# Two alternating scratch tiles, halved transfers, and layer 1's bias moved from a PSUM seed on ScalarE to an addition on VectorE, in a four-layer graph network

## The chip, the cores and the metric

The kernel runs on one core of a Trainium2 chip. The metric is the device time of one execution in microseconds. Besides it there is one profiled execution, in which every instruction of every engine has a start and an end.

## The reference

Thirty-two graphs go through four layers. A graph has 512 tokens `x` of width 256 and an adjacency `adj` of 512 x 512, everything in fp32. Each layer ends in `x = layernorm(x + layer(x, adj))`. The change touches layer 1 most:

```
layer 0:  relu(((1 + eps) x + adj x) W1 + b1) W2 + b2            (hidden width 512)
layer 1:  h = adj (x W^T + b);   h if h > 0 else alpha h
layer 2:  h = layernorm(x);      relu((adj h) W_rel + b_rel + h W_root), added to x
layer 3:  agg = eps x + adj x;   silu(rmsnorm(agg W1 + b1)) W2 + b2   (hidden width 1024)
```

In layer 1 the sum over the neighbours can be taken first: `adj (x W^T + b) = (adj x) W^T + rowsum(adj) b`. The kernel does it so, and `rowsum(adj) b`, the outer product of row sums and bias, is the term whose place the change moves.

## The kernel before

**Tiling.** A graph's tokens lie in one SBUF tile of 128 partitions x 4 chunks x 256 (a "room", 4 KB a partition; there are 37 of them, line 679). Matmuls are fp32 with 128 x 128 weights and a moving side of 256 or 128 columns. Most products of 2 x 2 blocks are done with seven block products instead of eight (`seven`, line 846), whose operand sums are VectorE's `room<-room` additions, and whose results are added up out of PSUM by VectorE (or copied by ScalarE where it is a first one).

**Transposes.** Layers 0 and 3 end in `dense_turned` (line 1092): the product comes out feature by token, VectorE transposes 32 x 32 squares, and `spread_squares` (line 1272) sends the squares through a scratch buffer in DRAM (`corner`): four transfers of 128 KB into it, one of 512 KB back (line 1282). `add_turned` (line 1131) then adds the result to `x` in two halves, each of which reads from the whole returned tile. Layer 2 needs its input turned and goes the like way with `gather_squares` (line 1285): four transfers out, four of 128 KB back. All these transfers are issued by SyncE, in order.

**Norms.** `Norm.half` (line 1177) lets ScalarE take sums and sums of squares of two chunks of 256: the activation's own output is not wanted and goes to one tile, `scrap` (line 836, written by `total`, line 735), only its accumulator counts. GpSimd takes the power -0.5 (`inv_sqrt`), and `Norm.put` (line 1210) scales each chunk on VectorE or on ScalarE, whichever the planner picks.

**Layer 1** (line 1398). With `SEED = 1` ScalarE first writes `b_1` times the row sum of each token into the PSUM bank (line 1421), two instructions for each half, and the matmuls of `dense_tok` (line 997) accumulate on top. Then ScalarE takes `relu(-ps)`, and VectorE makes the leaky activation and the residual with two scalar_tensor_tensor instructions (lines 1431 and 1432).

**The order of the work** is not left to a scheduler of the language. Every operation is recorded (`Plan.do`, `Plan.move`) with its operands and a cost from small formulas (lines 33 to 95): busy time and latency for the engines, wire time and lateness for the transfers. `Plan.order` (line 479) then plays the kernel through with these costs: always the operation that can start first, among those by rank, the rank being graph number times `period` plus due time (`RULES`, `SHIFT`); a tile or bank is taken when the plan holds it free. Up to five graphs are in flight (`FLIGHT`). It fixes, for all 32 graphs, the order of instructions on each engine, the tile each uses, and, where an operation has two ways, the engine (`YIELD` is a surcharge on VectorE there). `SPARE` is added to the landing of each transfer, `AHEAD` limits how far a later graph may run ahead. The instructions are issued in this order (line 1567); so every constant among these moves instructions of the whole kernel. Nearly all instructions are issued at line 366, all transfers at line 413.

Of the kernel before, what the change touches and what calls it, by code (L numbers as in the profile page):

```python
# [12 lines left out]
AF = mybir.ActivationFunctionType  # L13
ALU = mybir.AluOpType

P = 128
# [5 lines left out]
def span(ap):  # L22

    n = 1
    for d in ap.shape[1:]:
        n *= d
    return n
# [28 lines left out]
    return 0.035 + n * 0.00089 + columns * 0.113, 0.105  # L56


def total_time(n, columns):
    return 0.187 + n * 0.00089 + columns * 0.1, 0.1  # L60

# [8 lines left out]

SPARE = 0.8


KEEP = 0.4
# [3 lines left out]
    return 0.1 + kbytes / 450, 1.0  # L80


LOAD, BLOCK = (0.9, 1.7), (0.3, 0.67)
KEPT, BACK = (0.2, 0.6), (0.35, 0.93)
CORNER, PIECES = (0.46, 0.8), (0.65, 1.05)
TURNED, QUARTER = (2.1, 0.63), (0.58, 0.98)
LINE, SPREAD, RESULT = (0.22, 0.1), (1.47, 0.81), (1.36, 0.8)

GENTLE = 2.7

HAND = dict(tensor=0.12, vector=0.09, scalar=0.09, gpsimd=0.14, sync=0.1)
WEIGHTS, AGAIN = 0.09, 0.09
# [15 lines left out]
SOON = 0.03  # L110


YIELD = 0.6

# [2 lines left out]

RULES = [(37, 1.8, 19, 0.7)]

SHIFT = {-1: -19, 0: 12, 1: 3, 2: 2, 3: -1, 5: 1, 30: -8, 31: -18}
HALVES = 2
AHEAD, LAST = 86.0, 500.0
TURN = {0:(2,3),2:(99,0),3:(0,3)}
ROWS = 1  # L130
ONE = 0
PLAIN = 0
ONTO = ()
SEED = 1
BEHINDS = 1


# [143 lines left out]
class Plan:  # L281
# [60 lines left out]
    def do(self, out, *ways, ordered=None, scrap=None, behind=()):  # L342


        ins = list(behind)
        port = False
        def first(x):
            ap = x.model if isinstance(x, Part) else x
            return ap.offset // ap.ap[0][0] if ap.ap[0][0] else 0
        crosses = False  # L350
        for e, method, _, args, kw in ways:
            tiles = [x for x in (*args, *kw.values()) if isinstance(x, (bass.AP, Part))]
            ins += tiles
            in_psum = any(isinstance(x, Part) and x.room.pool.psum for x in tiles)
            crosses |= e == "vector" and any(first(x) != first(out) for x in tiles)
            port |= e == "gpsimd" or method in TWO_OPERANDS and not in_psum

        def issue(engine, method, args, kw):
            def put(x):
                return x.place() if isinstance(x, Part) else x  # L360

            kw = {k: put(x) for k, x in kw.items()}
            if scrap is not None:
                kw["accum_out"] = put(out)
            to = put(out) if scrap is None else scrap
            getattr(getattr(self.nc, engine), method)(to, *(put(x) for x in args), **kw)  # L366

        self.add(
            {
                e: (times, lambda e=e, m=method, args=args, kw=kw: issue(e, m, args, kw))  # L370
                for e, method, times, args, kw in ways
            },
            out, ins, ordered, port, crosses=crosses,
        )
# [267 lines left out]
def tile_gnn_stack(ctx: ExitStack, tc: tile.TileContext, a: dict, out: bass.AP):  # L642
# [25 lines left out]
    nc = tc.nc  # L668
    B, N, D = a["x"].shape
# [6 lines left out]
    HC = NC // 2  # L676
    TH = N // 2
    FH = FC3 // 2
    FLIGHT, ROOMS, SMALL = 5, 37 - ONE, 10

    const = ctx.enter_context(tc.tile_pool(name="const", bufs=1))
    work = ctx.enter_context(tc.tile_pool(name="work", bufs=1))
# [37 lines left out]
    def scalar(func, n, x, times=scalar_time, **kw):  # L720
        columns = sum(k in ("scale", "bias") and not isinstance(v, float) for k, v in kw.items())
        return "scalar", "activation", times(n, columns), (x,), dict(func=func, **kw)
# [10 lines left out]
        plan.do(o, scalar(func, span(o), x, **kw))  # L733

    def total(o, x, func, **kw):
        plan.do(o, scalar(func, span(x), x, times=total_time, **kw), scrap=scrap)

    def copy(o, x):
        plan.do(o, scalar(AF.Copy, span(o), x), vector("tensor_copy", span(o), x))
# [38 lines left out]
    def bank(*shape, onto=False, sums=True):  # L778

        n = 1
        for d in shape:
            n *= d
        return Part(Room(banks, sums=n * sums, onto=n * onto)).shaped(*shape)
# [4 lines left out]
    def half(t, h):  # L790
        return t[:, h * HC : (h + 1) * HC]
# [16 lines left out]
    def constant(name, shape):  # L808
        return const.tile(shape, F32, tag=name, name=name)
# [23 lines left out]
    ident = constant("ident", [P, P])  # L833
    make_identity(nc, ident)
    mhalf = constant("mhalf", [P, N // Q])
    scrap = constant("scrap", [P, D])
    nc.vector.memset(scrap, 0.0)
    nc.vector.memset(mhalf, -0.5)
    pause = constant("pause", [P, 48])
    nc.vector.memset(pause, 0.0)  # L840
# [324 lines left out]
    class Norm:  # L1165
# [33 lines left out]
        def finish(self, h, m, plus, place):  # L1199

            mine = slice(h * HC, (h + 1) * HC)
            ve, rstd, shift = self.ve[:, mine], self.rstd[:, mine], self.shift[:, mine]
            ts(ve, self.squares[:, mine], m / self.n, plus, ALU.mult, ALU.add)
            inv_sqrt(rstd, ve)
            mul(shift, self.less[:, mine], rstd)
            for c in range(h * HC, (h + 1) * HC):
                self.put(c, self.r, rstd[:, c % HC : c % HC + 1], shift[:, c % HC : c % HC + 1])
            plan.move(place, half(self.r, h), (RESULT[0] / 2, RESULT[1]), into=f"out{plan.graph}{h}")

        def put(self, c, y, scale, shift):  # L1210
            r = self.r[:, c, :]
# [60 lines left out]
    def spread_squares(of):  # L1272

        to = room(P // Q, NC * DC * Q)
        of, via = of.whole(P // Q, NC * DC * Q), next(corners)
        names = [f"{via.tensor.name}{a}" for a in range(P // Q)]
        places = via.rearrange("(b i) (a x) -> a i b x", i=Q, a=P // Q)
        for a, name in enumerate(names):  # L1280
            plan.move(places[a], of[a * Q : (a + 1) * Q], CORNER, into=name)
        plan.move(to.whole(N * DC), via, TURNED, outof=names)
        return to

    def gather_squares(to, of):
# [64 lines left out]
    def load_x(b):  # L1350
        x = tok()
        src = a["x"][b].rearrange("(p c) d -> p c d", c=NC)
        for h in range(2):
            plan.move(half(x, h), half(src, h), LOAD, gentle=b > 0)
        return x

    def aggregate_first(x, adjacency):
# [40 lines left out]
    def layer1(x, adjacency):  # L1398

        rows = adjacency.row_sums()  # L1400
        aT = aggregate(x, adjacency)
        rs = small(NC)
        by_token(rs, column_sums(rows), 1.0, None, ALU.mult)
        v, neg = tok(), tok()
        norm = Norm(v)

        def done(h):
            act(half(neg, h), half(v, h), AF.Relu, scale=-1.0)
            stt(half(x, h), half(neg, h), nalpha, half(x, h), ALU.mult, ALU.add)
            stt(half(v, h), half(v, h), 0.0, half(x, h), ALU.max, ALU.add)  # L1410
            norm.half(h)

        if ONE:
            for c in range(NC):
                act(v[:, c, :], b_1, AF.Copy, scale=rs[:, c : c + 1])
            dense_add(v, dense_sums(*([halves(aT[:, k : k + 1])] for k in range(DC))), A_1, done, "one")
        for h in range(0 if ONE else 2):
            if SEED:
                ps = dense_tok(
                    [(aT[:, k, :], W_1[:, k, :]) for k in range(DC)], h,  # L1420
                    lambda o, c: plan.do(o, scalar(AF.Copy, D, b_1, scale=rs[:, c : c + 1]), behind=[aT] if BEHINDS else []),
                )
                got = ps
            else:
                ps = dense_tok([(aT[:, k, :], W_1[:, k, :]) for k in range(DC)], h)
                for i in range(HC):
                    c = h * HC + i
                    stt(v[:, c, :], b_1, rs[:, c : c + 1], ps[:, i, :], ALU.mult, ALU.add)
                got = half(v, h)
            act(half(neg, h), got, AF.Relu, scale=-1.0)  # L1430
            stt(half(x, h), half(neg, h), nalpha, half(x, h), ALU.mult, ALU.add)
            stt(half(v, h), got, 0.0, half(x, h), ALU.max, ALU.add)
            norm.half(h)

        norm.scales((1.0 + LN_EPS, LN_EPS * LN_EPS), (0.25, 0.25 * LN_EPS))
        h = norm.scaled(0)
        xx = norm.scaled(1)
        u = tok()
        for c in range(NC):
            if ROWS:  # L1440
                act(u[:, c, :], shift_rel, AF.Copy, scale=rs[:, c : c + 1])
            else:
                stt(u[:, c, :], shift_rel, rs[:, c : c + 1], shift_2, ALU.mult, ALU.add)
        if ROWS:
            plus_row(u, shift_2)
        return h, xx, u
# [21 lines left out]
    def layer3(x, adjacency, b):  # L1468
# [27 lines left out]
        if b < B - HALVES:  # L1496
            if turn:
                add_turned(x, dense_turned(right, A2_3, b2c_3), norm.half)
            else:
                dense_add(x, right, A2_3, norm.half)  # L1500
            norm.scales((1.0, LN_EPS))
            y = norm.scaled()
            plan.move(place, y, RESULT, into=f"out{b}", gentle=b < B - 4)
        else:

            def done(h):
                norm.half(h)
                norm.finish(h, 1.0, LN_EPS, half(place, h))

            dense_add(x, right, A2_3, done)  # L1510
# [1 line left out]


    plan.graph = -1
    idle, zeros = bank(D), scrap
    for _ in range(9):
        mm(idle, zeros[:, 0:P], zeros, True, True)
    eps0 = row("L0_gnn_eps")
# [2 lines left out]
    loop0 = constant("loop0", [P, P])  # L1521
    ts(loop0, ident, one_eps0, None, ALU.mult)
    plan.graph = 0
    x = load_x(0)
    adjacency = Adjacency(0)
    W1_0 = weight("L0_gnn_W1")
# [83 lines left out]
```

## Time and profile before

| | |
|---|---|
| median of 3 runs | 2293.68 us (2291.74 to 2293.85) |
| the profiled execution's own time | 2292.24 us |
| its span, first to last instruction | 2290.4 us |
| TensorE's granted clock | 0.999 |
| ScalarE into PSUM for layer 1's bias (128x256) | x128, 477 ns each, 60.8 us busy |
| VectorE scaling a chunk in `Norm.put` (128x256) | x176, 405 ns each |
| ScalarE scaling a chunk in `Norm.put` (128x256) | x464, 595 ns each |
| DMA queue | 29.6% of 16 engines, 193.35 MB |

A page of the profile gives for each engine its busy time, the share of the span, and the number of instructions. PE is TensorE's matmul and PEld its weight load, which lies beside matmuls; DVE is VectorE, ACT ScalarE, POOL GpSimd, SP SyncE. One fp32 matmul of the program leaves two matmul records and two weight loads. A group of instructions is told by line, engine, operation, output<-inputs and shape, with its number, busy time, mean duration of one, and the idle time ahead of it with what ended it. In the table of waits a row says who waited for whom, in all, how often, and at most. In a timeline like instructions that follow each other are merged ("x22").

### The profile page before, as it was taken

To read this page: it belongs to the slowest core of one execution; us is meant where nothing else is said; L and a number is where in the kernel's file an instruction comes from. 1 tells how busy PE (TensorE), PEld (TensorE's weight loads), DVE (VectorE), ACT (ScalarE), POOL (GpSimd) and SP (SyncE) were. 2 spreads that over 40 slices of the span, in tenths; PEclk is the share of its full clock that TensorE was granted. 3 is DMA by queue.
4 is the path that set the end of the run, shared out by engine and by line. 5 is a ranking of instruction groups with operands and counts; after the bars stand their busy time and mean duration, and the time that the engine had idled before them with its cause. 6 is when DMAs were issued, how large, how long until landed. Compare 5 with 4: busy or idle time off the path is not lost.

```text
span 2290.4 us, 37068 instructions
## 1 busy us (share of the span) xinstructions
PE 2275.2 (99%) x11694; PEld 2012.6 (88%) x11694; DVE 2121.8 (93%) x5404; ACT 1762.2 (77%) x4733; POOL 240.5 (11%) x168
## 2 busy tenths in 40 slices
PE   9999999999999999999999999999999999999998
PEld 8889888888888888888888888888888888888888
DVE  8989998999999999999999999999999999998988
ACT  4777778777787777877778877778777887768785
POOL 0000101111011110111100111101111011101111
PEclk9999999999999999999999999999999999999999
DMA  8011322243321333323333223332133331333101
GB/s 246 26 31 40 106 83 75 69 111 106 105 71 54 109 107 106 85 52 94 111 96 112 46 80 111 106 104 77 49 109 109 86 106 51 95 90 84 42 15 61
DMA packets 268404, 195.71 MB, mean 85 GB/s; under 512 B 144560, under 2 KB 224176, under 8 KB 268208
## 3 DMA queue, kind: packets, MB, share of 16 engines
q1 hardware_dynamic: 268208, 193.35, 29.6%
q8 instruction: 93, 1.52, 0.3%
q14 instruction: 103, 0.84, 0.1%
HBM read 124.27 MB, written 69.01 MB: 84 GB/s over the span
## 4 chain that ended last, share of the span: by engine, by line
PE 82%; DVE 8%; ACT 5%; DMA 2%; issue 1%; SPq 1%; POOLq 0%; POOL 0%; DVEq 0%; ACTq 0%
PE ps L366 82%; DVE room L366 7%; ACT room L366 3%; ACT scrap L366 2%; DMA room<-corner 1%; SPq L413 1%; DMA corner<-room 1%; DVE few L366 0%; ACT ps L366 0%; DMA room<-in_x_dram 0%; DVE few L391 0%; DVE A L366 0%; DMA line<-few 0%; POOLq L1606 0%; DVE pause L1571 0%
## 5 line engine op out<-in xcount | busy, mean ns | idle before, releaser
L366 PE MATMUL ps<-room,room 128*128 128x256 f32 (+1 forms) x3572 | 925.9, 381 | 3.5 <-DVE room L366 1.9
L366 DVE TENSOR_TENSOR room<-room,room 128x512 f32<-128x512 f32 (+1 forms) x1486 | 852.1, 601 | 14.7 <-ACT room L366 7.0
L366 PE MATMUL ps<-room,L_gnn_W 128*128 128x256 f32 x2848 | 751.7, 380 | 1.9 <-DVE room L366 1.7
L366 PEld LDWEIGHTS ps<-room,room 128*128 128x128 f32 x3572 | 654.0, 190 | 94.7 <-ACT room L366 8.0
L366 PEld LDWEIGHTS ps<-room,L_gnn_W 128*128 128x128 f32 x2848 | 535.6, 190 | 81.5 <-DVE room L366 5.7
L366 DVE TENSOR_TENSOR room<-ps,room 128x256 f32<-128x256 f32 (+1 forms) x1125 | 528.2, 485 | 70.3 <-PE ps L366 64.6
L366 PE MATMUL ps<-room,A 128*128 128x256 f32 x2136 | 563.6, 379 | 0.3 <-ACT room L366 0.2
L366 ACT ACTIVATE room<-ps,L_gnn_b_c 128x256 f32<-128x256 f32 x984 | 409.8, 469 | 73.6 <-PE ps L366 71.4
L366 POOL TENSOR_TENSOR few<-few,mhalf 128x4 f32<-128x4 f32 (+2 forms) x162 | 239.8, 1481 | 2045.4 <-DVE few L366 1680.8
L366 PEld LDWEIGHTS ps<-room,A 128*128 128x128 f32 x2136 | 403.5, 190 | 56.4 <-ACT room L366 1.9
L366 ACT ACTIVATE room<-ps 128x256 f32<-128x256 f32 (+1 forms) x577 | 227.6, 400 | 244.2 <-PE ps L366 239.2
L366 DVE TENSOR_TENSOR room<-room 128x256 f32<-128x256 f32 (+1 forms) x638 | 311.3, 494 | 16.6 <-ACT room L366 7.3
L366 ACT ACTIVATE scrap<-room,few 128x256 f32<-128x256 f32 x500 | 253.3, 507 | 67.5 <-DVE few L366 61.7
L366 ACT ACTIVATE room<-room,few 128x256 f32<-128x256 f32 x464 | 252.2, 595 | 29.1 <-DVE few L366 28.8
L366 ACT ACTIVATE scrap<-room 128x256 f32<-128x256 f32 x500 | 207.4, 415 | 52.7 <-DVE room L366 43.3
L366 ACT ACTIVATE room<-room 128x1024 f32<-128x1024 f32 x192 | 202.3, 1057 | 48.6 <-DVE room L366 47.6
L366 PE MATMUL ps<-L_gnn_W,room 128*128 128x256 f32 (+1 forms) x960 | 207.6, 331 | 0.7 <-DVE room L366 0.6
L366 ACT ACTIVATE room<-room,L_gnn_rms_weight_c 128x512 f32<-128x512 f32 x256 | 171.7, 722 | 4.2 <-DVE room L366 4.1
L366 PEld LDWEIGHTS ps<-L_gnn_W,room 128*128 128x128 f32 x960 | 156.4, 191 | 17.3 <-ACT ps L366 1.3
L366 PE MATMUL ps<-A,room 128*128 128x128 f32 x1104 | 155.4, 276 | 0.5 <-DVE room L366 0.4
L366 PEld LDWEIGHTS ps<-A,room 128*128 128x128 f32 x1104 | 147.5, 191 | 8.9 <-DVE room L366 2.4
L366 DVE STREAM_TRANSPOSE room<-room 128x512 f32<-128x512 f32 x168 | 113.8, 696 | 1.6 <-ACT room L366 0.5
(62 smaller groups left out, 1221.2 us busy)
## 6 DMA issues: line engine op xcount, KB each, us to landing
corner<-room SPq DMA_DIRECT2D x336, 128.0 KB, 2.5
room<-in_adj_dram SPq DMA_DIRECT2D x128, 256.0 KB, 5.6
room<-corner SPq DMA_DIRECT2D x54, 512.0 KB, 3.8
room<-in_x_dram SPq DMA_DIRECT2D x64, 256.0 KB, 5.8
room<-corner SPq DMA_DIRECT2D x120, 128.0 KB, 3.0
out_dram<-room SPq DMA_DIRECT2D x30, 512.0 KB, 4.7
room<-in_adj_dram SPq DMA_DIRECT2D x128, 64.0 KB, 2.0
diagonal<-room SPq DMA_DIRECT2D x62, 128.0 KB, 2.1
```

What stands on the lines that cost most here:

```text
L366: getattr(getattr(self.nc, engine), method)(to, *(put(x) for x in args), **kw)
L413: getattr(self.nc, engine).dma_start(to, of, **kw)
```

## The change

1. **Layer 1's bias.** `SEED = 0`: no seed by ScalarE; the matmuls start the bank themselves, and VectorE writes `v = b_1 * rowsum + ps` for each chunk of 256 out of PSUM into a room. Relu and the activation after it read this room instead of the bank.
2. **Scratch.** `scrap` becomes two tiles which the sums of the norms use in turn; one room less is there (36).
3. **Transfers.** The 512 KB transfer at the end of `spread_squares` becomes two of 256 KB; each waits for two of the four that filled the scratch buffer. The result of a graph goes out as two transfers of 256 KB instead of one of 512 KB (the last two graphs did so before).
4. **The planner's constants** are changed with it: transfer costs (the load of x has its own now), `SPARE`, `YIELD`, `GENTLE`, `RULES`, `SHIFT`, `AHEAD`. With them the order on every engine is another one.

The built instructions of the two kernels, counted by kind, differ thus: TensorE none in number or shape (5861 instructions each); VectorE 128 more scalar_tensor_tensor 128x256 from PSUM, 64 of 128x512 that read SBUF in place of PSUM, 129 fewer chunk scalings, 3 fewer copies, 14 fewer filler memsets; ScalarE 128 fewer seeds, 64 Relu of 128x512 reading SBUF in place of PSUM, 129 more chunk scalings, 3 more copies; SyncE 84 more transfers (54 for the squares, 30 for results).

```diff
-SPARE = 0.8
+SPARE = 1.2
...
-LOAD, BLOCK = (0.9, 1.7), (0.3, 0.67)
-KEPT, BACK = (0.2, 0.6), (0.35, 0.93)
-CORNER, PIECES = (0.46, 0.8), (0.65, 1.05)
-TURNED, QUARTER = (2.1, 0.63), (0.58, 0.98)
-LINE, SPREAD, RESULT = (0.22, 0.1), (1.47, 0.81), (1.36, 0.8)
+LOAD, LOAD_X, BLOCK = (0.86, 1.8), (0.67, 1.4), (0.3, 0.66)
+KEPT, BACK = (0.31, 0.5), (0.33, 0.94)
+CORNER, PIECES = (0.43, 0.84), (0.61, 1.09)
+TURNED, QUARTER = (0.75, 1.05), (0.59, 1.05)
+LINE, SPREAD, RESULT = (0.22, 0.1), (1.45, 0.83), (0.66, 1.1)
...
-GENTLE = 2.7
+GENTLE = 2.8
...
-YIELD = 0.6
+YIELD = 0.9
...
-RULES = [(37, 1.8, 19, 0.7)]
+RULES = [(33, 1.6, 15, 0.6)]
...
-SHIFT = {-1: -19, 0: 12, 1: 3, 2: 2, 3: -1, 5: 1, 30: -8, 31: -18}
+SHIFT = {-1: -19, 0: 12, 1: 3, 2: 5, 26: 3, 27: -1, 31: -11}
...
-AHEAD, LAST = 86.0, 500.0
+AHEAD, LAST = 93.0, 500.0
...
-SEED = 1
+SEED = 0
...
-            to = put(out) if scrap is None else scrap
+            to = put(out) if scrap is None else next(scrap)
...
-    FLIGHT, ROOMS, SMALL = 5, 37 - ONE, 10
+    FLIGHT, ROOMS, SMALL = 5, 36, 10
...
-        plan.do(o, scalar(func, span(x), x, times=total_time, **kw), scrap=scrap)
+        plan.do(o, scalar(func, span(x), x, times=total_time, **kw), scrap=scraps)
...
-        plan.move(to.whole(N * DC), via, TURNED, outof=names)
+        for h in range(2):
+            mine = slice(h * N * DC // 2, (h + 1) * N * DC // 2)
+            plan.move(to.whole(N * DC)[:, mine], via[:, mine], TURNED, outof=names[2 * h : 2 * h + 2])
...
-            plan.move(place, y, RESULT, into=f"out{b}", gentle=b < B - 4)
+            for h in range(2):
+                plan.move(half(place, h), half(y, h), RESULT, into=f"out{b}{h}", gentle=b < B - 4)
```

The branch that `SEED = 0` takes was in the kernel already:

```
                for i in range(HC):
                    c = h * HC + i
                    stt(v[:, c, :], b_1, rs[:, c : c + 1], ps[:, i, :], ALU.mult, ALU.add)
                got = half(v, h)
            act(half(neg, h), got, AF.Relu, scale=-1.0)
            stt(half(x, h), half(neg, h), nalpha, half(x, h), ALU.mult, ALU.add)
            stt(half(v, h), got, 0.0, half(x, h), ALU.max, ALU.add)
```

More of the change, by code (lines that the diff above doesn't have):

```diff
@@ L56, in scalar_time, with seed_time @@
     return 0.035 + n * 0.00089 + columns * 0.113, 0.105
+def seed_time(n, columns):
+    return 0.15 + n * 0.00089 + columns * 0.113, 0.105
 def total_time(n, columns):
@@ L835, in tile_gnn_stack @@
     mhalf = constant("mhalf", [P, N // Q])
-    scrap = constant("scrap", [P, D])
-    nc.vector.memset(scrap, 0.0)
+    scraps = [constant(f"scrap{i}", [P, D]) for i in range(2)]
+    nc.vector.memset(scraps[0], 0.0)
     nc.vector.memset(mhalf, -0.5)
@@ L1207, in finish @@
                 self.put(c, self.r, rstd[:, c % HC : c % HC + 1], shift[:, c % HC : c % HC + 1])
-            plan.move(place, half(self.r, h), (RESULT[0] / 2, RESULT[1]), into=f"out{plan.graph}{h}")
+            plan.move(place, half(self.r, h), RESULT, into=f"out{plan.graph}{h}")
         def put(self, c, y, scale, shift):
@@ L1353, in load_x @@
         for h in range(2):
-            plan.move(half(x, h), half(src, h), LOAD, gentle=b > 0)
+            plan.move(half(x, h), half(src, h), LOAD_X, gentle=b > 0)
         return x
@@ L1420, in layer1 @@
                     [(aT[:, k, :], W_1[:, k, :]) for k in range(DC)], h,
-                    lambda o, c: plan.do(o, scalar(AF.Copy, D, b_1, scale=rs[:, c : c + 1]), behind=[aT] if BEHINDS else []),
+                    lambda o, c: plan.do(o, scalar(AF.Copy, D, b_1, times=seed_time, scale=rs[:, c : c + 1]), behind=[aT] if BEHINDS else []),
                 )
@@ L1514, in tile_gnn_stack @@
     plan.graph = -1
-    idle, zeros = bank(D), scrap
+    idle, zeros = bank(D), scraps[0]
     for _ in range(9):
@@ L1523, in tile_gnn_stack @@
     plan.graph = 0
+    scraps = cycle(scraps)
     x = load_x(0)
```

## The prediction

> **What bounds the kernel now.** I read the page's first part, then the matmuls by form, a stretch of TensorE's timeline, the tables of waits, and the chain that ended last.
>
> ```profile
> PE 2275.2 (99%) x11694; PEld 2012.6 (88%) x11694; DVE 2121.8 (93%) x5404; ACT 1762.2 (77%) x4733; POOL 240.5 (11%) x168
> ...
> 702.18 4.91 PE L366 MATMUL ps<-room,room 128*128 128x256 f32 x22
> 706.93 1.03 PE L366 MATMUL ps<-room,L_gnn_W 128*128 128x256 f32 x4
> ...
> 763.43 1.05 PE L366 MATMUL ps<-L_gnn_W_root,room 128*128 128x128 f32 x8
> 764.32 0.39 PE L366 MATMUL ps<-L_gnn_W_rel,room 128*128 128x128 f32 x2
> ```
>
> From one start to the next, 22 records (11 matmuls) of 256 columns took 706.93 - 702.18 = 4.75 us, 0.4318 a matmul; 8 records (4 matmuls) of 128 columns took 0.89, 0.2225 each; one of 512 columns counts twice 256, 0.864. By form the trace has 9078, 2600 and 16 records, half as many matmuls: 4539 x 0.4318 + 1300 x 0.2225 + 8 x 0.864 = 2256.1 us. That is what TensorE needs without a pause; the span is 2290.4, so **34.3 us are all that any reordering can win**, and the change leaves TensorE's matmuls as they are.
>
> A rule speaks for more: the Trainium skill, Perfetto Trace Analysis, "Identifying the Most-Contended Engine", says that matmul busy time is a poor measure of TensorE's headroom and names the weight loads' busy share instead. That share is 88%, which would leave 12%, 278 us. The row decides: at this pitch TensorE starts the next matmul as soon as it can, with gaps between the weight loads all the same. I take 34.
>
> Where are the 34? I counted the matmuls by form in 40 equal stretches and subtracted their pitch from each stretch. A stretch without any pause comes out at -0.35 (records cut by its edges count twice), which I add back: 0 to 114.5 us 7.4; 114.5 to 1946.8 us 9.5; 1946.8 to 2233.1, where the last graphs drain, 8.4; the last 57 us 8.4, of which the end after the last matmul (2283.4) is 7.0. Between about 687 and 916, or 1374 and 1546, there is nothing: the steady state is at the floor. The pauses of the middle have addresses:
>
> ```profile
> 249.23 3.84 DMA corner<-room
> 253.14 5.55 DMA room<-corner
> ...
> 610.33 3.06 DMA room<-corner
> ...
> 961.51 3.30 DMA room<-corner
> ...
> 1314.13 5.77 DMA room<-corner
> ...
> DVE few L366 <- ACT scrap L366: 19.0, 28, 2.0
> PEld ps L366 <- DVE room L366: 14.5, 38, 1.5
> PEld ps L366 <- ACT room L366: 13.5, 44, 0.8
> DVE room L366 <- DMA room<-corner: 6.6, 9, 1.4
> PEld ps L366 <- ACT ps L366: 1.6, 5, 0.5
> ```
>
> The chain leaves TensorE for transposed squares coming back from DRAM, about 1595 and 1667 us too. VectorE waits for such a landing nine times, 6.6 us in all, and in the six stretches around these places the pauses are 1.5 + 1.0 + 0.8 + 1.7 + 0.65 + 1.1 = 6.75 us. So of 9.5 us in the middle, 6.75 are late squares that VectorE passes on to TensorE.
>
> **The change part by part.** *Layer 1's bias.* ScalarE loses 128 x 0.477 = 61.1 us. VectorE gains 128 scalar_tensor_tensor of 128x256 from PSUM with a column as scalar; the trace has none. Lower end: the plain addition from PSUM, 0.416. Upper: the 128x512 form with a column, 0.745, less 256 columns (0.681 - 0.416) = 0.48, which I take since it is the same form: 61.4 us. The scaled chunks that move (129, as the built orders show) take 129 x 0.405 = 52.2 off VectorE and put 129 x 0.595 = 76.8 on ScalarE; three copies and 14 fillers fewer are -2.6. The 64 (max, add) read SBUF for PSUM: 0.680 against 0.682, nothing. Relu from SBUF is nearest to the 256-wide pair 0.415 against 0.375, +0.04 x 64 = 2.6. Sums: **VectorE +6.6 us** (93%), ScalarE +18. Cover is VectorE's 168.6 us of idle time: cost 0; without cover +6.6. TensorE's waits for the seed, 1.6 us, go; behind a seed stood its bank, held before its first matmul, and what is late next is the operand `aT`. I take -1 (0 to -1.6).
>
> *Scratch.* In the trace one accumulator read and what follows it:
>
> ```profile
> 2263.17 0.19 ACT L366 ACTIVATION_READ_ACCUMULATOR scrap<-room,few 128x1 f32 x1
> 2263.38 0.42 ACT L366 ACTIVATE scrap<-room 128x256 f32<-128x256 f32 x1
> 2263.71 0.18 ACT L366 ACTIVATION_READ_ACCUMULATOR scrap<-room 128x1 f32 x1
> 2263.80 3.16 ACT L366 ACTIVATE room<-room,L_gnn_rms_weight_c 128x512 f32<-128x512 f32 x5
> ```
>
> An activation into another tile starts 0.09 us after the read's start, one into the same tile 0.21: writing `scrap` again costs 0.12. In the built order 414 of 467 neighbouring pairs carry a wait for ScalarE itself: some 50 us, less than the 528 that ScalarE idles, so nothing for its load; but each norm's half, four sums, comes out up to 0.4 earlier, and VectorE waited 19 us for these sums. TensorE feels it only through "ACT room" and "DVE room". I take -0.8 (0 to -3).
>
> *Transfers.* The return was 512 KB, 3.8 us from issue to landing (128 KB: 2.1 to 3.0); 256 KB, about 3. It waited for the fourth of four fills; now the first half waits for two. The second still waits for the fourth and lands last: 3.0 + 0.4 of SyncE's issue against 3.8, a gain of some 0.4. `add_turned` reads both halves at once, so an early first half gains nothing. Here a rule speaks against: the Trainium skill, DMA: Bandwidth & Descriptors, "Anatomy of one DMA", fits about 2.0 us fixed per transfer plus bytes at 436 GB/s, for another issue path. For 512 KB it gives 3.2, for 256 KB 2.6; it agrees with the rows that most of a transfer is fixed, and charged in series it would add 54 x 2.0 = 108 us of latency. SyncE's rows show transfers in flight together, so I charge only the issue: 84 x 0.41 = 34 us of SyncE, which waits over 1000 us for VectorE. What stands behind in its queue, the loads for later graphs, comes 0.4 to 0.8 later, on 5.6 us.
>
> More than that does the distance do. Summing VectorE's rows in the built orders from the transposition of the squares to the first instruction that reads them back: for layer 2's gathered squares before mostly 9.8 to 10.9 us, after mostly 10.7 to 12.1; for the spread ones before 9.4 at the short end, after 9.7. Gathered squares thus get 1 us more and spread ones about 0.3 and a landing 0.4 sooner, against lateness on VectorE of 0.6 to 1.4. That removes the smaller waits fully and most of the others: I take -5.4 of 6.75 (0 to -6.75).
>
> *Order and rooms.* The ends (8.4 while draining, 7.4 at the start) are ordered anew; no row says how well. Cold start and the end after the last matmul, 10 us together, stay. One room of 37 fewer can delay loads. I bound it by -8 and +10, and take -1, near zero.
>
> Sum: -1 - 0.8 - 5.4 - 1 = -8.2. The profiled execution took 2292.24, 1.84 over its span and 1.44 under the median: 2284.0 on its scale, 2285.5 on that of the median 2293.68.
>
> **The rivals.** *Slower: VectorE's eviction becomes what TensorE waits for.* Between layer 1's last matmul and its norm stood a Relu out of PSUM; now two evictions of 0.48 come ahead of it on an engine that is 93% busy, where in-order work of three other graphs stands around them: 0.96 us later per half. It decides if the slack to layer 2's first sums is under that. Against it: TensorE's waits for VectorE are 38 in all, most graphs have none. For it: slack is not visible in a wait table. If half of it comes through once in each of some 26 steady graphs: 26 x 0.48 = +12.5, 2306. Chance 0.22.
>
> *No change.* Late squares are replaced by others: two halves are queued on SyncE where eight fills already took 5.9 us at 602 us, and the drain loses what the middle wins: 2293 (2289 to 2298). Chance 0.18.
>
> *More.* The drain improves too: a further 8 of the 15.8 us at both ends, 2277. Chance 0.14.
>
> *The scratch does not do what it says:* 384 neighbouring sums still carry a wait for ScalarE in the built order, perhaps for the sum before the last, perhaps for the last. Then 0.8 is lost: 2286.3, within the forecast.
>
> **How the numbers follow.** Forecast (2280 to 2289) 0.46, more 0.14, no change 0.18, slower 0.22. A measurement here tells 0.2%, 4.6 us. Faster: 0.46 + 0.14 less a little = 0.59; within 0.2%: 0.18; slower 0.23. The range reaches from 2273, near the floor with both ends' 10 us (2256.1 + 10 + the 3.3 from span to median = 2269), to 2303, where half the slower case is left out.
>
> **What would show it.** Right: no pause at `room<-corner` in the middle, VectorE busy at 2125 to 2132, sums into scratch 0.5 apart instead of 0.62, no "ACT ps". Wrong: a pause in every graph or every second one, at "DVE room" behind layer 1; or a drain after 1946 us that costs more than 8.4.

## The result, and the profile after

The changed kernel takes 2281.0 us (median of 5 runs, 2280.44 to 2282.45) against 2291.74 (5 runs, 2291.18 to 2293.85): a ratio of 0.9954, 95% interval 0.9942 to 0.9965, that is 10.7 us less. The forecast was 8.2 us less. The direction and the size of the sum came out well; what it is made of did not.

The profiled execution took 2282.45 us, with a span of 2280.7. First the engines' busy times of the page after:

```profile
PE 2265.3 (99%) x11694; PEld 2014.4 (88%) x11694; DVE 2120.5 (93%) x5386; ACT 1730.0 (76%) x4737; POOL 243.6 (11%) x168
```

TensorE's busy time fell with the span; its instructions are the same, so what fell is pauses: 2280.7 - 2256.1 = 24.6 us are left of 34.3. VectorE is where it was, and ScalarE lost 32 us. The chain that ended last, of the kernel before and then of the changed one:

```profile
PE 82%; DVE 8%; ACT 5%; DMA 2%; issue 1%; SPq 1%; POOLq 0%; POOL 0%; DVEq 0%; ACTq 0%
```

```profile
PE 94%; DVE 2%; DMA 2%; ACT 1%; issue 0%; SPq 0%; POOL 0%; ACTq 0%; DVEq 0%
```

The end now hangs on TensorE itself for 94% of the span, and on ScalarE for 1% in place of 5%. The table of waits after:

```profile
PEld ps L370 <- DVE room L370: 12.9, 30, 2.0
DVE few L370 <- ACT scrap L370: 10.6, 15, 1.3
DVE room L370 <- DMA diagonal<-room: 6.2, 8, 2.4
DVE room L370 <- DMA room<-corner: 4.2, 5, 1.3
PEld ps L370 <- ACT room L370: 3.4, 9, 0.9
```

TensorE's weight loads wait for ScalarE's rooms 3.4 us instead of 13.5, and no longer for the seed. VectorE waits for late squares 4.2 us instead of 6.6. The row for `diagonal` was 0.6 us before: VectorE wants to overwrite the diagonal blocks before they have been saved to DRAM. That wait has grown tenfold; the longest, 2.4 us, ends at 355.4 us, and SyncE's issue of the transfer took 2.0 us from 349.0.

Where TensorE pauses, by the sum of the prediction (matmuls by form times their pitch, taken off each stretch) over four long stretches. "Drain" is the 286.3 us that end 57.3 us before the end of the span. Records that an edge of a stretch cuts count twice, so a figure can be up to 0.5 us low:

| kernel | 0 to 114.5 us | middle | drain | last 57.3 us |
|---|---|---|---|---|
| before | 6.9 | 10.3 | 8.2 | 8.0 |
| changed | 6.3 | 6.0 | 2.2 | 9.3 |
| changed, one scratch tile (e1) | 6.5 | 20.9 | 5.6 | 10.6 |
| before, halves (e5) | 7.7 | 6.2 | 7.2 | 8.0 |
| before, two scratch tiles (e9) | 5.1 | 7.9 | 1.1 | 7.8 |
| before, both (e10) | 5.8 | 5.0 | 1.3 | 8.0 |

So the gain has two places: 4.3 us in the middle, and 6.0 us in the drain, for which the prediction had taken 1 together with the start.

### The profile page after: what moved, and what is told of

It reads as the page before. It is cut to its first block, busy times and chain, and to the rows that moved or that the text cites. A ratio compares the mean times of both kernels' runs of the same rounds, so it can differ in the third digit from the quotient of the medians.

```text
span 2280.7 us, 37259 instructions
## 1 busy us (share of the span) xinstructions
PE 2265.3 (99%) x11694; PEld 2014.4 (88%) x11694; DVE 2120.5 (93%) x5386; ACT 1730.0 (76%) x4737; POOL 243.6 (11%) x168
## 4 chain that ended last, share of the span: by engine, by line
PE 94%; DVE 2%; DMA 2%; ACT 1%; issue 0%; SPq 0%; POOL 0%; ACTq 0%; DVEq 0%
PE ps L370 94%; DVE room L370 2%; DMA diagonal<-room 1%; ACT room L370 1%; DMA room<-in_x_dram 0%; DMA room<-in_adj_dram 0%; DMA L_gnn_W<-in_L_gnn_W_dram 0%; SPq L417 0%; DVE few L370 0%; ACT scrap L370 0%; POOL few L370 0%; DVE few L395 0%; ACTq L1614 0%; DVE pause L1579 0%; DVEq L370 0%
## 5 line engine op out<-in xcount | busy, mean ns | idle before, releaser
L370 PE MATMUL ps<-room,room 128*128 128x256 f32 (+1 forms) x3572 | 942.2, 381 | 4.3 <-DVE room L370 3.8
L370 PE MATMUL ps<-room,A 128*128 128x256 f32 x2136 | 585.2, 379 | 0.1
L370 DVE TENSOR_TENSOR room<-ps,room 128x256 f32<-128x256 f32 (+1 forms) x1125 | 517.2, 482 | 54.4 <-PE ps L370 49.4
L370 POOL TENSOR_TENSOR few<-few,mhalf 128x4 f32<-128x4 f32 (+3 forms) x162 | 242.9, 1503 | 2031.5 <-DVE few L370 1356.1
L370 ACT ACTIVATE room<-ps 128x256 f32<-128x256 f32 x516 | 196.6, 383 | 268.6 <-PE ps L370 263.8
L370 ACT ACTIVATE room<-room,few 128x256 f32<-128x256 f32 x593 | 316.0, 595 | 28.0 <-DVE few L370 27.8
L370 ACT ACTIVATE room<-room 128x1024 f32<-128x1024 f32 (+1 forms) x256 | 240.7, 951 | 29.7 <-DVE room L370 26.3
L370 PEld LDWEIGHTS ps<-A,room 128*128 128x128 f32 x1104 | 158.1, 191 | 10.9 <-DVE room L370 1.1
L370 PE MATMUL ps<-A,room 128*128 128x128 f32 x1104 | 165.0, 275 | 0.4 <-DVE room L370 0.4
L370 DVE TENSOR_TENSOR room<-room,loop 128x256 f32<-128x256 f32 (+1 forms) x256 | 105.6, 416 | 22.4 <-PE ps L370 9.9
```

## The experiments

The planner makes a new order whenever a cost changes, so an edit undone in the plain way undoes the order with it. The experiments are of two kinds: those that keep the order of instructions on every engine, and change only what the machine does at one place (e1, e2, e5, e9, e10), and those in which the plan is made anew (e3, e4, e6, e7, e8, e11, e12). My theory was that of the prediction: the new order, with more distance between a transfer and its reader, is most of the gain. The rivals were the scratch tiles, the halves, the eviction, and `SHIFT`.

All times are medians; the kernel before, run beside them on the same chip, took 2292.35 us (e1 to e4), 2292.34 (e5 to e8) and 2292.65 (e9 to e12).

| run | us | ratio to before, 95% interval |
|---|---|---|
| e1 changed, one scratch tile, order kept | 2303.18 | 1.0050 (1.0038 to 1.0063) |
| e2 changed, whole squares, order kept | 2283.45 | 0.9960 (0.9948 to 0.9973) |
| e3 old code, new constants | 2368.19 | 1.0333 (1.0319 to 1.0347) |
| e4 new code, old constants | 2342.05 | 1.0215 (1.0201 to 1.0229) |
| e5 before, halves, order kept | 2287.89 | 0.9984 (0.9975 to 0.9993) |
| e6 changed, seed on ScalarE | 2339.43 | 1.0206 (1.0192 to 1.0220) |
| e7 before, eviction on VectorE | 2386.87 | 1.0411 (1.0397 to 1.0426) |
| e8 changed, old SHIFT | 2299.85 | 1.0034 (1.0022 to 1.0047) |
| e9 before, two scratch tiles, order kept | 2282.44 | 0.9954 (0.9941 to 0.9966) |
| e10 before, two scratch tiles and halves, order kept | 2279.04 | 0.9938 (0.9926 to 0.9951) |
| e11 changed, SPARE 1.25 | 2295.52 | 1.0012 (1.0003 to 1.0021) |
| e12 before, SPARE 0.85 | 2329.76 | 1.0159 (1.0145 to 1.0173) |

**e1, one scratch tile in the new order.**

```diff
-    scraps = cycle(scraps)
+    scraps = cycle(scraps[:1])
```

> The changed kernel with its order of instructions, tiles and transfers kept to the last one, but all sums of the norms write one scratch tile again. My theory (the order is what gains, the scratch only 0.8 us): 2281 to 2283, with ScalarE's neighbouring sums 0.62 apart again. Rival (the chain's waits of VectorE on these sums were what TensorE paid for, so the scratch is a main part): 2285 or more, with TensorE waiting for ScalarE's and VectorE's rooms as before.

2303.18 us: with one scratch tile the changed kernel loses 22 us and is slower than the kernel before. The theory had allowed 2. The chain of e1:

```profile
PE 53%; DVE 21%; ACT 19%; DMA 3%; issue 3%; SPq 1%; ACTq 0%; DVEq 0%; POOL 0%
```

ScalarE stands in it with 19%, against 1% with two tiles, though its busy share is 77%. The pauses lie all through the middle (20.9 us against 6.0), and they come again with each graph: the chain runs along ScalarE for 4.9 us from 713, 855, 997 and 1139 us on. Which sums feed that place was not followed.

**e2, whole squares in the new order.** The first half's issue is left out, and the second's place issues the whole.

```diff
+            whole = lambda: nc.sync.dma_start(to.whole(N * DC).place(), via)
-            plan.move(to.whole(N * DC)[:, mine], via[:, mine], TURNED, outof=names[2 * h : 2 * h + 2])
+            plan.move(to.whole(N * DC)[:, mine], via[:, mine], TURNED, outof=names[2 * h : 2 * h + 2], what=whole if h else None)
```

> The changed kernel with its order kept, but the squares come back in one transfer of 512 KB issued where the second half stood. My theory (a landing 0.4 us later and nothing more, since the addition needs both halves): 2281 to 2284, a few more waits for the squares. Rival (halving is a main part): 2285 or more. Rival (halving costs, as a fixed price for each transfer would have it): below 2280.5.

2283.45 us, within the theory's range. Its interval overlaps that of the changed kernel (0.9948 to 0.9973 against 0.9942 to 0.9965), both profiled spans are 2280.7 us, and VectorE waits 3.0 us for squares against 4.2. In this order the halves bring nothing that these runs can tell.

**e3 and e4, code and constants exchanged.** The planner's constants (SPARE, GENTLE, YIELD, RULES, SHIFT, AHEAD and the transfer costs; in e3 also 36 rooms) of one kernel with the code of the other.

```diff
-SPARE = 0.8
+SPARE = 1.2
...
-TURNED, QUARTER = (2.1, 0.63), (0.58, 0.98)
+TURNED, QUARTER = (1.5, 1.05), (0.59, 1.05)
...
-RULES = [(37, 1.8, 19, 0.7)]
+RULES = [(33, 1.6, 15, 0.6)]
```

> The kernel before (seed on ScalarE, one scratch tile, whole transfers) with the planner's constants of the changed kernel (the whole transfers costed as two halves) and 36 rooms, so a new order for the old instructions. My theory (order and distances are most of it): 2282 to 2287. Rival (the three named edits are it, constants only follow them): 2290 or more.

> The changed kernel's code (eviction on VectorE, two scratch tiles, halves) with the planner's constants of the kernel before (halves costed at half the wire time), so another order. My theory: 2288 to 2296, with late squares in the middle and a drain that pauses 6 to 9 us as before. Rival (the named edits are it): 2280 to 2284.

2368.19 and 2342.05 us: both far over either kernel. e3 lies within its rival's open range (2290 or more), e4 over both ranges. At face value neither "the order is it" nor "the edits are it" fits both; how little such a kernel can tell, e11 and e12 show below.

**e5, halves in the old order.**

```diff
+            n = span(to) // pieces
+            for i in range(pieces):
+                t, o = (to, of) if pieces == 1 else (x[:, i * n : (i + 1) * n] for x in (to, of))
+                getattr(self.nc, engine).dma_start(t, o, **kw)
-            getattr(self.nc, engine).dma_start(to, of, **kw)
```

> The kernel before with its order kept, but each return of the squares is issued as two transfers of 256 KB one behind the other. My theory (the second half lands about when the whole did, up to 0.4 us sooner; half of the late squares are of this kind): 2290 to 2292, VectorE's waits for the squares 5 to 7 us. Rival (halving by itself takes the late squares away): 2287 or less. Rival (each transfer pays a fixed price in series): over 2294.

2287.89 us, 4.4 less than before: more than my theory gave to the halving by itself, a little less than the rival. The middle pauses 6.2 us instead of 10.3. VectorE's two kinds of reader of returned squares, before and after this edit (the first reads spread squares, which are halved, the second gathered ones):

```profile
L366 DVE TENSOR_TENSOR room<-room,room 128x512 f32<-128x512 f32 x1040 | 676.8, 681 | 8.8 <-DMA room<-corner 3.4 <-ACT room L366 2.4
L366 DVE TENSOR_TENSOR room<-room 128x512 f32<-128x512 f32 x192 | 129.9, 682 | 12.7 <-ACT room L366 5.8 <-DMA room<-corner 3.3 <-DMA room<-in_adj_dram 1.5
```

```profile
L366 DVE TENSOR_TENSOR room<-room,room 128x512 f32<-128x512 f32 x1040 | 677.9, 683 | 6.7 <-ACT room L366 2.4 <-DMA room<-corner 1.2
L366 DVE TENSOR_TENSOR room<-room 128x512 f32<-128x512 f32 x192 | 130.0, 683 | 11.9 <-ACT room L366 5.8 <-DMA room<-in_adj_dram 2.6 <-DMA room<-corner 2.3
```

The halved kind waits 1.2 us instead of 3.4, the other kind, whose transfers are as before, 2.3 instead of 3.3. Together that is 3.5 us of 6.6, less than the 5 to 7 expected; but ScalarE now waits 3.5 us for returned squares, which it did not before. A half takes 3.5 us from issue to landing in this run (median), against 3.8 for the whole. In 29 of 54 pairs the first half is issued before the last fill has landed, and from that landing to the pair's it takes 3.96 us (median) instead of 4.26.

**e6 and e7, the eviction undone and done alone.** `SEED = 1` in the changed kernel, `SEED = 0` in the kernel before; the plan is made anew.

```diff
-SEED = 0
+SEED = 1
```

> The changed kernel with the bias put into PSUM by ScalarE again, all constants kept (the plan is made anew, so the order moves somewhat). My theory (the seed is worth 1 us): 2281 to 2284. Rival (the seed, in that TensorE waited for ScalarE, is a main part): 2286 or more.

> The kernel before with the bias added by VectorE at the eviction and nothing else (the plan is made anew with the old constants). My theory: 2289 to 2293, TensorE's waits for ScalarE into PSUM gone and the late squares still there. Rival (the eviction is a main part): 2286 or less. Rival (VectorE becomes late): over 2296.

2339.43 and 2386.87 us. The two contradict each other as prices: the eviction would win 58 us by the one and lose 95 by the other. In e6 weight loads wait 25.7 us for seeds, in e7 82.8 us for ScalarE's rooms and 29.3 for VectorE's (before: 13.5 and 14.5). e7 lies in the range of the rival that VectorE becomes late, and so does not rule it out; the larger part of its waits names ScalarE.

**e8, the old SHIFT.**

```diff
-SHIFT = {-1: -19, 0: 12, 1: 3, 2: 5, 26: 3, 27: -1, 31: -11}
+SHIFT = {-1: -19, 0: 12, 1: 3, 2: 2, 3: -1, 5: 1, 30: -8, 31: -18}
```

> The changed kernel with the SHIFT of the kernel before, which moves graphs at the start and at the end only. Theory that the drain was won by the new SHIFT: the stretch after 1937 us pauses 7 us or more instead of 2.2, and the time is 2285 to 2288. Theory that the drain was won by the other constants or by the code: 2280 to 2283.

2299.85 us; the drain pauses 8.9 us instead of 2.2, as the SHIFT theory said, but the middle loses another 10 (16.2 against 6.0), most of it between 344 and 574 us, where the start's SHIFT still acts. It is a new order as a whole, so it doesn't single out the drain; the time lies over both ranges.

**e9 and e10, the scratch tiles alone, then with the halves, in the old order.** Two fp32 tiles do not fit beside 37 rooms, so both are bf16; the sums themselves stay fp32, and one activation with its sum takes as long as with an fp32 scratch (503 and 410 ns against 504 and 414 in the changed kernel). One bf16 tile alone was not run; but the changed kernel's two fp32 tiles give sums 0.40 and 0.49 us apart just as the two bf16 tiles do, so the number of tiles is what counts.

```diff
-    scrap = constant("scrap", [P, D])
+    scraps = cycle([const.tile([P, D], BF16, tag=f"scrap{i}", name=f"scrap{i}") for i in range(2)])
+    scrap = rooms.tiles[-1][:, 0:D]
...
-            to = put(out) if scrap is None else scrap
+            to = put(out) if scrap is None else next(scrap)
```

> The kernel before with its order kept and two scratch tiles for the sums (in bf16, since two in fp32 do not fit beside 37 rooms; nobody reads them). The new order lost 22 us with one scratch tile. If the scratch is worth that much in any order: 2275 or less. If only an order that was made for a ScalarE without that wait feels it: 2288 to 2292.

> The kernel before with its order kept, with both physical edits: two scratch tiles and the squares coming back in two halves. Theory that the physical edits give the gain and the new order little more: 2279 to 2284. Theory that the new order with its drain is half of it: 2285 to 2288.

2282.44 and 2279.04 us. Two scratch tiles alone take 10.2 us off the kernel before, nothing else touched; with the halves it is 13.6, close to the sum of both alone (10.2 + 4.4). Both of e9's expectations missed: it is not 22, and it is not nothing. e10 lies at the lower end of its first theory, that the physical edits give the gain and the new order little more.

Most of it can be read at one place. In the drain many norms come together. ScalarE's timeline before:

```profile
2058.80 0.42 ACT L366 ACTIVATE scrap<-room 128x256 f32<-128x256 f32 x1 [0.32 <-ACT scrap L366]
2059.13 0.19 ACT L366 ACTIVATION_READ_ACCUMULATOR scrap<-room 128x1 f32 x1
2059.34 0.42 ACT L366 ACTIVATE scrap<-room 128x256 f32<-128x256 f32 x1
2059.67 0.19 ACT L366 ACTIVATION_READ_ACCUMULATOR scrap<-room 128x1 f32 x1
2059.89 0.51 ACT L366 ACTIVATE scrap<-room,few 128x256 f32<-128x256 f32 x1
...
2065.12 0.51 ACT L366 ACTIVATE scrap<-room,few 128x256 f32<-128x256 f32 x1
```

And the same twelve sums, in the same order, in e9:

```profile
2052.14 0.42 ACT L366 ACTIVATE scrap<-room 128x256 bf16<-128x256 f32 x1 [0.47 <-ACT scrap L366]
2052.47 0.19 ACT L366 ACTIVATION_READ_ACCUMULATOR scrap<-room 128x1 f32 x1
2052.56 0.40 ACT L366 ACTIVATE scrap<-room 128x256 bf16<-128x256 f32 x1
2052.87 0.19 ACT L366 ACTIVATION_READ_ACCUMULATOR scrap<-room 128x1 f32 x1
2052.96 0.49 ACT L366 ACTIVATE scrap<-room,few 128x256 bf16<-128x256 f32 x1
...
2057.19 0.51 ACT L366 ACTIVATE scrap<-room,few 128x256 bf16<-128x256 f32 x1 [0.17 <-DVE few L366]
```

From the first start to the twelfth: 6.32 us before, 5.05 after, of which 0.17 is a wait that ScalarE only now meets because it is early. From the first of these sums on, 28.4 us before and in e9; the columns are the window, its length, the busy time and number of instructions of PE, PEld, DVE, ACT and POOL, TensorE's granted clock, the DMA engines' share and GB/s:

```profile
2058.80:2087.20 28.40, 27.79 (x154) 23.29 (x152) 25.19 (x69) 27.66 (x86) 4.02 (x3) 1.00 0.21 48
```

```profile
2052.14:2080.50 28.36, 28.36 (x166) 25.64 (x165) 27.34 (x75) 28.12 (x96) 4.02 (x3) 1.00 0.20 48
```

ScalarE is busy nearly all the time in both, but gets 96 instructions done in e9 where it got 86 before, and TensorE no longer pauses. Before, the chain that ended last runs along ScalarE; at this place of the chain before, and then of e9:

```profile
2061.69 0.61 ACT scrap L366 x2
2062.33 0.52 ACT scrap L366 x2
2062.87 0.61 ACT scrap L366 x2
2063.50 0.52 ACT scrap L366 x2
```

```profile
2040.90 43.30 PE ps L366 x258
```

In e9 the chain from 2041 to 2084 us is TensorE alone. The drain's pauses fall from 8.2 to 1.1 us. The wait of weight loads for ScalarE's rooms in the drain, before and in e9:

```profile
PEld ps L366 <- ACT room L366: 6.5, 17, 0.6
```

```profile
PEld ps L366 <- ACT room L366: 0.7, 2, 0.4
```

The rest of the gain, 2.4 us in the middle and 1.8 at the start, was not followed to its places.

**e11 and e12, a nudge.** The assumed landing of every transfer 0.05 us later.

```diff
-SPARE = 1.2
+SPARE = 1.25
```

> The changed kernel with SPARE 1.25 for 1.2, a change of 0.05 us in the assumed landing of each transfer, nothing else. If an order is good because its constants fit the machine: 2280 to 2284. If the constants were picked to hit one good order among many bad ones: 2290 or more, and then the kernels with mixed constants say nothing of the edits they undo.

> The kernel before with SPARE 0.85 for 0.8, nothing else. If the constants fit the machine: 2290 to 2296. If they pick one good order among many: 2305 or more.

2295.52 and 2329.76 us, 14.5 and 37 over the kernels that they nudge. Both nudges, too small to matter as costs, hit worse orders; so a kernel whose plan was made anew can't price an edit below some tens of us. e8's loss (19 us over the changed kernel) is in the range of what a nudge does. Those of e3, e4, e6 and e7 (58 to 95 us over the kernel whose code they start from) are larger than both nudges, but what part of them is the edit's and what the order's these runs can't tell. Where e12 loses is one stretch above all, 114 to 348 us, with 18.4 us of pauses; more than half is a single wait there for a power on GpSimd:

```profile
PEld ps L366 <- POOL few L366: 11.0, 1, 11.0
```

Part of the loss is TensorE's clock. From 150.1 to 163.8 us, which begins within this wait, the granted clock is 0.50 (the columns are as above):

```profile
150.10:163.80 13.70, 6.88 (x31) 6.48 (x32) 11.09 (x25) 5.27 (x8) 1.01 (x1) 0.50 0.00 1
```

The 23 matmuls of 128 columns from 158.04 us on, the last of them already at full clock again, take 7.95 us, where the pitch at full clock gives 5.1. Counted by the matmuls in such stretches and their pitch, the half clock costs some 7 us in e12 and some 10 in e4 and in e7 (an estimate from the traces). The two kernels and the runs with the order kept have no such stretch before the last 25 us.

## Why the prediction was right, and where it was wrong

**Right.** *The bound.* TensorE's pitch left 34.3 us and no more; 24.6 are left now, of which the two ends take most. *Single durations.* The eviction takes 473 ns (taken: 0.48), Relu from SBUF 629 ns (taken: 0.63):

```profile
L370 DVE SCALAR_TENSOR_TENSOR room<-L_gnn_b,few,ps 128x256 f32<-128x256 f32 x128 | 56.2, 473 | 1.2 <-PE ps L370 0.8
L370 ACT ACTIVATE room<-room 128x512 f32<-128x512 f32 x64 | 40.3, 629 | 3.3 <-DVE room L370 3.2
```

*The engines' sums came out less well.* ScalarE's +18, with the 50 us of the scratch taken off, would be -32, and it went from 1762.2 to 1730.0; but e1 puts the scratch at 40.8 us of busy time (1770.8 against 1730.0), and so the rest at +8.6: two errors that cancel. VectorE was to gain 6.6 and lost 1.3, outside the 2125 to 2132 us foretold. Mean durations count the overlap of neighbours twice: by the busy column the eviction is 0.44 each, not 0.48, and the moved chunks are 49.2 us, not 52.2, which leaves some +4; the other 5 us lie in overlaps that were not followed. *The slower rival.* In the order that was built nothing shows of it: weight loads wait for VectorE's rooms 12.9 us, 30 times, against 14.5, 38 times, and the middle pauses 6.0 us where the rival needed 12.5 more than before. *That the scratch may not do what it says.* It does: neighbouring sums start 0.40 and 0.49 apart in e9 where it was 0.54 and 0.63.

**Wrong: the scratch's term.** The step read: "some 50 us, less than the 528 that ScalarE idles, so nothing for its load", and it took -0.8 with -3 as the far end. e9 measures -10.2 on the order for which the sum was made. The 0.12 us per sum was right: with them ScalarE's busy time goes from 1762.2 to 1726.5 us in e9. What failed is the cover: 528 us is ScalarE's idle time over the whole kernel, while in the drain, where the norms come thickest and 7.1 of the 10.2 us are won, it has hardly any (27.7 of 28.4 us busy). The chain before runs along ScalarE there, from 2059 to 2087 us, half of it in sums; that was at hand, and I had read the chain for its transfers only. In the new order the same step fails in the middle too (e1), at a place of every graph.

**Wrong in attribution: -5.4 for late squares, and "more than that does the distance do".** The middle did lose 4.3 us of pauses, but in the old order the halving alone gets 4.1 there (e5), and the scratch tiles alone, which leave the squares as late as they were (6.9 us), 2.4 (e9). The step had put the halving at 0.4 us a landing and little in the sum. The 0.4 itself was fair (0.3 in e5); that a few tenths are enough because VectorE is only 0.6 to 1.4 late and TensorE has no slack behind it fits the rows, but is argued. In the new order halving shows nothing (e2), so the gains do not add. The late squares are fewer, but not gone, as the sign of being right asked: VectorE still waits 4.2 us for them in the changed kernel, 3.0 in e2 and 3.5 in e5. No run has the distance alone. The new order also brought more late transfers of another kind (`diagonal`).

**Wrong: that the new order wins.** Its step, -1 between -8 and +10, stood for the ends. The drain is mainly the scratch tiles': in the old order they leave 1.1 of its 8.2 us (e9), in the new one 3.4 of the 6.0 us come back with one tile (e1). Adding up: two edits in the old order give 13.6 us, the changed kernel 10.7. The eviction and the new order together thus show no gain, perhaps a loss of some 3 us; the intervals (0.9926 to 0.9951 and 0.9942 to 0.9965) overlap, so e10 at 2279.04 us is the fastest kernel run here, but not shown to be faster than the changed one. What the order costs depends on the scratch: with one tile (e1) the new order is 10.8 us slower than the kernel before, halves and eviction included. That the forecast came near is luck, owed to two errors of opposite sign: the scratch nine too small, and all other terms (-7.4 in sum, where beside the scratch's 10.2 some -0.5 is left) seven too large.

**Open.** What the eviction on VectorE is worth by itself: with it in, the plan is another, and a nudge alone moves the time by more than its price. A kernel that keeps the old order and evicts on VectorE would need a place for the added instructions, which is a choice of its own; it wasn't tried. Why one scratch tile costs 22 us in the new order and 10 in the old. What the halving of the results' transfers does: no run undoes it or does it alone. Why an order loses 15 to 95 us when its constants are moved was followed only to the waits and the clock named above.

## What to carry to other kernels

Price a small wait by the stage in which it is thickest, not by the engine's idle time over the kernel: an engine at 77% can be what the chain hangs on for some 28 us. And busy time is not all work: with the same instructions in the same order, ScalarE was busy 36 us less once neighbouring sums could overlap (e9). When a planner or scheduler stands between an edit and the machine, keep the instruction order and change one physical thing; and nudge a constant first, to learn how large a change means nothing. Where two remedies act on the same wait, do not add their gains.

## What the runs showed of the hardware that was not expected

An activation whose output goes to the same tile as the last one's starts 0.21 us after the read of the accumulator began, one to another tile 0.09: 0.12 us a sum for a result that nobody reads, 10.2 us of kernel time here in one order and 22 in another; the page counts it as busy time. And a return of 256 KB from DRAM takes 3.2 to 3.5 us where 512 KB take 3.8, yet two of them, the first of which waits for two fills and not for four, took 2.2 us off VectorE's waits for these squares (e5).
